# A transformer decoder on one core: scores kept together behind the outputs, paired projections later in their step

## The chip, the cores and the metric

The kernel runs on one core of one Trainium2 chip. The metric is the device time of one execution in microseconds (us). Several executions are timed, and their median is compared. One further execution is recorded by the hardware profiler. The core has five engines that run side by side, each with its own queue of instructions, which it takes in the built order: PE (TensorE, matrix products; its weight loads are shown as PEld), DVE (VectorE), ACT (ScalarE), POOL (GpSimd) and SP (SyncE, which issues DMA transfers). ACT issues transfers too. Results of PE land in PSUM banks, from where DVE or ACT copy them.

## The reference, cut to what matters

The program is a decoder of two layers on 8 sequences of 128 tokens with 512 features. The change lies in the last attention of it, the cross attention of layer 1, which is

```python
hidden = jnp.concatenate([context, latents], axis=1)       # 128 + 128 tokens
q = (latents @ Wq.T).reshape(b, q_len, H, HD)              # H = 16 heads of 96
k = (hidden @ Wk.T).reshape(b, s_len, KV, HD)              # KV = 4 groups
v = (hidden @ Wv.T).reshape(b, s_len, KV, HD)
...
scores = jnp.einsum('bkgqd,bksd->bkgqs', q, k) * scale
attn = jax.nn.softmax(scores.astype(jnp.float32), axis=-1).astype(q.dtype)
out = jnp.einsum('bkgqs,bksd->bkgqd', attn, v)
...
return out @ Wo.T
```

followed by `x = layernorm(x + ...)` and a low-rank mixture (`L1_ffn`), again with a residual and a norm.

## The kernel before, in words

The cross attention goes in steps, one for each sequence b (0 to 7), in the loop at line 1212. A step has two halves `hh` of 8 heads each. For each half it makes:

- the scores (`Heads8.__init__`, line 971): 24 matmuls of 32 x 128 by 256 columns in 6 rounds of four row groups, into two PSUM tiles of two banks each. PE runs each matmul as two instructions, so a half has 48. Both two-bank tiles are taken by one half.
- the softmax: maxima on DVE (`maxima`, line 986), exponentials on ACT (line 997), reciprocals, scaling and 32 x 32 transposes on DVE (`exps`, lines 1001 to 1005), in two sub-halves of four heads.
- the turn (`turn`, line 1011): 16 DMAs of 64 KB that bring the probabilities into the tile `pT`. The first half's go out on SP, the second half's on SP and ACT in turn.

The outputs of step b - 1 (`mixed`, line 1021) are computed in step b: three groups `o_x` of 8 matmuls, each into one bank, copied to `oTx` by DVE (groups 0 and 2) or ACT (group 1). There are four single banks, used by all results other than scores.

Between these, `Front` makes values (`pvx`), keys (`pkx`) and queries (`pqx`) of the next pair of sequences in pieces, which `nxt.go(n)` takes from a list. `LOWS` lists pieces of the low-rank mixture of earlier sequences.

The output projection of sequences 0 to 3 is done in pairs (`paired`, line 1043): sequences 0 and 1 in step 2, sequences 2 and 3 in step 4. Seven products of 6 matmuls (12 PE instructions) take the place of eight. In order: product 1 of the first operand, copied to `p1` by ACT (line 1073); product 2 of `s`, copied to `p5` by ACT (line 1074); product 3; product 4 of `s` after DVE has subtracted from it (line 1051); product 5 of a half of `oTx` after DVE has subtracted `s` from that; products 6 and 7. The weight blocks for the products, 42 blocks of 128 KB, stream through three slots of 1 MB (`w_X_o`): after the last block of a slot is read, ACT issues the load of the slot's next content (`stream`, line 945). Blocks 0 to 23 are there when the pair starts, 24 to 41 come during it; block 24 is the first of product 5. After the pair, the slots are filled for the next pair, or with the plain weights (`plain_outputs`, line 950) for the later sequences, which are projected one at a time (line 1038).

The order on each engine is made by a planner when the program is built: it takes the recorded work and may put an instruction ahead of others that were recorded before it, within the data dependences. `tc.issue_after(x)` is an order edge: what is recorded inside is not placed ahead of x. In the built order of before, in steps 2 and 4, the scores of the second half, which are recorded after the pair, stand partly ahead of it: one round's half between the first and second group of outputs, one between the second and third, one behind the third, and the other 18 of the 24 matmuls behind the seven products.

Of the kernel before, what the change touches and what calls it, by code (L numbers as in the profile page):

```python
# [18 lines left out]
B, S, D = 8, 128, 512  # L19
# [24 lines left out]
def decoder(ctx: ExitStack, tc: tile.TileContext, a: dict, out: bass.AP):  # L44
    nc = tc.nc
# [475 lines left out]
    for n, (p, f) in enumerate(steps):  # L521
# [4 lines left out]
        for j in range(2):  # L526
            toks = slice(j * P, (j + 1) * P)
            of = lambda i, w, p=p, f=f, j=j: vs[p, j][i].rearrange("p a x d -> p (a x d)")[:, f * w : (f + 1) * w]
            units.append((qT[:, toks], kbd[:, :, toks], lambda of=of: of(0, 192), lambda of=of: of(1, 128)))
        now = Heads16(ap, units, causal_bias, oTs[p][:, :, f, :], f"a0_{p}_{f}")  # L530
# [318 lines left out]
    front = Front(0)  # L849
    turned = prev = oT_before = None  # L850
    keys_late = []
    for b in range(B):
# [3 lines left out]
        for f in (0, 2):  # L856
# [4 lines left out]
            now = Heads16(ap, units, alibi_bias(f), oT[:, f : f + 2, :], f"a1_{b}_{f}", keys_late)  # L861
# [57 lines left out]
    def form_sums():  # L919
        for t in slots:  # L920
            b11, b12, b21, b22 = (t[:, j * 512 : (j + 1) * 512] for j in range(4))
            nc.vector.tensor_tensor(b11, b12, b11, ALU.subtract)
            nc.vector.tensor_tensor(b12, b22, b12, ALU.subtract)
            nc.vector.tensor_tensor(b22, b22, b11, ALU.subtract)
            nc.vector.tensor_tensor(b21, b21, b22, ALU.subtract)
# [28 lines left out]
    with stage("x1b", 2, side="right") as ap, stage("f1", 2, side="right") as fp:  # L954
# [60 lines left out]
        def mixed(b, v, pT, oT):  # L1015

            for n in range(NS):
                po = bank(f"o_x1_{b}_{n}")
                for s in range(2):
                    for g in range(KV):  # L1020
                        nc.tensor.matmul(  # L1021
                            po[32 * g : 32 * g + 32, :],
                            lhsT=v[:, s, g * XD + 32 * n : g * XD + 32 * n + 32],
                            rhs=pT[:, s].rearrange("p i h x -> p (i h) x")[:, :, 64 * g : 64 * g + 64],
                            start=(s == 0), stop=(s == 1),
                        )
                (nc.scalar.copy if n == 1 else nc.vector.tensor_copy)(  # L1027
                    oT[:, n, :].rearrange("p (h i t) -> p i h t", h=4, i=4),
                    po.rearrange("p (i h t) -> p i h t", i=4, h=4),
                )  # L1030
# [12 lines left out]
        def paired(b0, b1):  # L1043

            o0, o1 = oTs_x.pop(b0), oTs_x.pop(b1)
            x0, x1 = xs[b0], xs[b1]
            first, second = slice(0, 256), slice(256, 512)
            s = ap.tile([P, NS, 256], F32, tag="s", name=f"s_x1_{b0}", bufs=1)
            p1, p5 = (ap.tile([P, 256], F32, tag=f"p{i}", name=f"p{i}_{b0}", bufs=1) for i in (1, 5))
            r0, r1 = (xp.tile([P, D], F32, tag="x", name=f"x_x1_{b}") for b in (b0, b1))  # L1050
            add = lambda eng, o, l, r, op=ALU.add: eng.tensor_tensor(o, l, r, op)
            used = [0]

            def product(left):
                ps = bank(f"pox_{b0}_{used[0]}")[:, :256]
                for kk in range(6):
                    h, n = divmod(kk, NS)
                    t, u = divmod(used[0], 8)
                    nc.tensor.matmul(  # L1059
                        ps, lhsT=left[:, n, h * P : (h + 1) * P], rhs=slots[t % 3][:, u * 256 : (u + 1) * 256],  # L1060
                        start=kk == 0, stop=kk == 5,
                    )
                    used[0] += 1
                    if u == 7:
                        if t < 3:
                            stream(t + 3)
                        elif t < 5 and not paired.last:
                            stream(t - 3)
                return ps

            add(nc.vector, s, o1[:, :, first], o1[:, :, second])
            add(nc.vector, o1[:, :, first], o0[:, :, first], o1[:, :, first], ALU.subtract)
            nc.scalar.copy(p1, product(o0[:, :, first]))
            nc.scalar.copy(p5, product(s))
            add(nc.vector, s, s, o0[:, :, first], ALU.subtract)
            add(nc.vector, x0[:, first], x0[:, first], p1)
            add(nc.vector, r0[:, first], product(o0[:, :, second]), x0[:, first])
            add(nc.vector, o0[:, :, second], o0[:, :, second], s, ALU.subtract)
            add(nc.vector, p1, product(s), p1)
            add(nc.vector, x0[:, second], x0[:, second], p5)  # L1080
            add(nc.vector, x0[:, second], x0[:, second], p1)
            add(nc.vector, r0[:, second], product(o0[:, :, second]), x0[:, second])
            add(nc.vector, x1[:, second], x1[:, second], p5)
            add(nc.vector, p1, product(o1[:, :, first]), p1)
            add(nc.vector, x1[:, first], x1[:, first], p1)
            add(nc.vector, r1[:, second], x1[:, second], p1)
            add(nc.vector, r1[:, first], product(o1[:, :, second]), x1[:, first])
            if paired.last:
                plain_outputs()
            else:  # L1090
                stream(2)
            for b, r in ((b0, r0), (b1, r1)):
                mean, rs = moments(r, f"x1_{b}")
                nc.vector.tensor_scalar(r, r, mean, rs, ALU.subtract, ALU.mult)
                xs[b] = r
# [95 lines left out]
        def outputs(b):  # L1191
            oTs_x[b] = ap.tile([P, NS, 512], F32, tag="oT", name=f"oTx_{b}", bufs=2)
            mixed(b, vs_x.pop(b), pTs.pop(b), oTs_x[b])
# [9 lines left out]
        PAIRED = 4  # L1203
# [8 lines left out]
        for b in range(B):  # L1212
            pr, j = divmod(b, 2)
            if j == 0 and b:
                front, nxt = nxt, upcoming
            toks = slice(j * P, (j + 1) * P)
            for hh in range(2):
                now = Heads8(front.qT[:, :, toks], front.kT[:, :, :, toks], 2 * hh, f"x1_{b}_{hh}")
                now.maxima()
                now.exps(0)  # L1220
                now.exps(1)
                if b < B - 2 and hh == 0:

                    if b > PAIRED:
                        nxt.go((4, 3)[j] if b < B - 3 else 2)
                        mix(b - 1)
                    elif b and not j:
                        nxt.go(4)
                        outputs(b - 1)
                        paired.last = b == PAIRED  # L1230
                        paired(b - 2, b - 1)
                    else:
                        nxt.go((4, 3)[j])
                        if b:
                            outputs(b - 1)
                    pTs[b] = pT_tile(b)
                    now.turn(pTs[b])
                    if b < 2:
                        with tc.issue_after(now.exp.ins):
                            keep_sums() if b else bring_weights()  # L1240
                elif b < B - 2:
                    if j == 1 and b < B - 3:

                        upcoming = Front(pr + 2)
                    now.turn(pTs[b], (nc.sync, nc.scalar))
                    nxt.go(2)
                    if b < 2:
                        with tc.issue_after((now.exp if b else now.rows).ins):
                            if b:
                                for t in range(3):  # L1250
                                    stream(t)
                            else:
                                form_sums()
                    for piece in LOWS.get(b, ()):
                        piece()
                    if b < B - 3:
                        nxt.go((1, 2)[j])
                elif hh == 0:

                    if b == B - 2:  # L1260
                        front.go(3)
                    else:
                        projected(b - 2)
                    first = now
                else:
                    if b == B - 2:
                        low_turn(B - 6)
                        low_turn(B - 5)
                        outputs(b - 1)
                        low_last(B - 6)  # L1270
                        low_scores(B - 4)
                        low_last(B - 5)
                    else:
                        low_turn(B - 4)
                        outputs(b - 1)
                        low_tokens(B - 3)

                    pTs[b] = pT_tile(b)
                    for heads in (first, now):
                        heads.turn(pTs[b], (nc.sync, nc.scalar))  # L1280
            vs_x[b] = front.v[:, j]
# [240 lines left out]
```

## Time and profile before

| | |
|---|---|
| Median of 3 timed runs | 871.89 us (871.49 to 874.71) |
| The profiled execution | 871.16 us |
| Its span, first to last instruction | 869.4 us |
| Granted TensorE clock, mean | 0.996 of full |
| PE busy | 843.0 us, 97% of the span |
| Cross attention, step 2 | outputs from 605.12 us, pair from 613.09 to 631.42 us |
| Cross attention, step 4 | outputs from 693.22 us, pair from 701.24 to 719.57 us |

Times inside an execution count from the span's start. In a row of the timeline, the first number is the start, the second the length from the first start to the last end, then the engine (with a q behind it where its sequencer issues a DMA), the line, the operation, written and read tiles, shapes, the number of instructions and in brackets the idle time before it and what ended it. Matmuls overlap, so the distance from one start to the next is the price of a group, not its length. In a row of the windows, the columns are the stretch, its length, the busy time of PE, PEld, DVE, ACT and POOL with the number of instructions, the granted clock, the share of the DMA engines and GB/s.

### The profile page before, as it was taken

How to read it: one execution, taken by the hardware profiler on the slowest of the kernel's cores; microseconds unless marked ns; L12 is line 12 of the kernel's file. 1: busy time of each engine (PE TensorE's matmuls, PEld its weight loads, DVE VectorE, ACT ScalarE, POOL GpSimd, SP SyncE). 2: the span in 40 equal slices, each digit the busy share in tenths (PEclk: the TensorE clock that was granted, in tenths of full speed). 3: DMA queues.
4: the chain of work that ended last, by engine and by line, in shares of the span. 5: the costliest groups of instructions: out<-in, count | busy, mean ns of one | idle time of the engine just before them, and what ended most of it. 6: DMA issues, size and time to landing. Idle time of an engine off the chain costs nothing.

```text
span 869.4 us, 18203 instructions
## 1 busy us (share of the span) xinstructions
PE 843.0 (97%) x6554; PEld 538.6 (62%) x6554; DVE 562.4 (65%) x2252; ACT 365.4 (42%) x1531; POOL 202.3 (23%) x299
## 2 busy tenths in 40 slices
PE   9999999999899999999999999999999999999996
PEld 5776655655454455555555687875787677576454
DVE  3656687776868666777778512874565547458754
ACT  3876574654222136766666403142024202224310
POOL 2500243243535315555555300000000000000000
PEclk9999999999999999999999999999999999999999
DMA  8700000130300002000002001676652264322341
GB/s 329 310 2 26 2 13 14 50 110 4 143 13 0 25 0 98 2 1 2 2 2 76 2 25 58 189 230 179 197 165 58 55 165 169 82 58 49 88 95 37
DMA packets 35258, 67.99 MB, mean 78 GB/s; under 512 B 5984, under 2 KB 22496, under 8 KB 32992
## 3 DMA queue, kind: packets, MB, share of 16 engines
q1 hardware_dynamic: 23152, 41.13, 15.3%
q10 hardware_dynamic: 12016, 25.70, 9.6%
q8 instruction: 52, 0.85, 0.4%
q14 instruction: 38, 0.31, 0.1%
HBM read 44.78 MB, written 5.24 MB: 58 GB/s over the span
## 4 chain that ended last, share of the span: by engine, by line
PE 59%; DVE 21%; ACT 11%; POOL 3%; issue 2%; DMA 2%; SPq 1%; ACTq 1%; POOLq 0%; DVEq 0%
ACT e_a L197 6%; PE pqx L86 6%; PE pkx L86 4%; PE pvx L86 4%; PE pox L1059 4%; PE o_x L1021 4%; PE pq L86 4%; DVE e_a L184 3%; PE pk L86 3%; PE pv L86 3%; PE po L86 3%; PE s_x L976 3%; PE pt_a L228 2%; PE pox L1038 2%; PE pof L623 2%
## 5 line engine op out<-in xcount | busy, mean ns | idle before, releaser
L197 ACT ACTIVATE e_a<-e_a,m_a 128x128 f32<-128x128 f32 (+1 forms) x512 | 184.8, 364 | 98.4 <-DVE m_a L184 98.4
L997 ACT ACTIVATE e_x<-s_x,m_x 128x256 f32<-128x256 f32 x128 | 58.6, 485 | 123.2 <-DVE m_x L987 66.9
L197 ACT ACTIVATION_READ_ACCUMULATOR e_a<-e_a,m_a 128x1 f32 x512 | 97.1, 190 | 0.0
L86 PE MATMUL pqx<-xTx,w_X_q 128*128 128x256 f32 x384 | 85.0, 380 | 1.3 <-DVE rc L1123 1.3
L86 PEld LDWEIGHTS pqx<-xTx,w_X_q 128*128 128x128 f32 x384 | 72.5, 190 | 12.6 <-issue 3.0
L97 POOL TENSOR_TENSOR rs_x<-ve_x,neghalf 128x1 f32<-128x1 f32 x7 | 3.8, 547 | 274.2 <-DVE ve_x L95 255.2
L986 DVE TENSOR_REDUCE m_x<-s_x 128x4 f32<-128x1024 f32 x32 | 37.6, 1218 | 38.8 <-PE s_x L976 38.8
L211 POOL TENSOR_TENSOR e_a<-e_a,rc_a 128x512 f32<-128x512 f32 (+1 forms) x64 | 52.7, 845 | 35.1 <-DVE rc_a L208 18.8
L228 PE MATMUL pt_a<-ident,e_a 128*128 128x128 f32 x384 | 48.4, 273 | 2.3 <-DVE m_a L184 2.3
L228 PEld LDWEIGHTS pt_a<-ident,e_a 128*128 128x128 f32 x384 | 43.5, 140 | 11.2 <-issue 4.7
L976 PE MATMUL s_x<-kTx,qTx 32*128 32x256 f32 x768 | 50.0, 384 | 0.0
L184 DVE CUSTOM_DVE_ANT_0 e_a<-s_a,masks 128x128 f32<-128x128 f32 (+1 forms) x256 | 46.8, 253 | 4.7 <-PE s_a L165 3.3
L184 DVE CUSTOM_DVE_ANT_0 e_a<-s_a,alibi 128x128 f32<-128x128 f32 (+1 forms) x256 | 47.3, 253 | 1.4 <-PE s_a L165 1.3
L976 PEld LDWEIGHTS s_x<-kTx,qTx 32*128 32x128 f32 x768 | 39.0, 184 | 14.5 <-issue 11.6
L1021 PE MATMUL o_x<-pT_x,vx 128*32 128x512 f32 x384 | 43.7, 595 | 0.9 <-DVE oTx L1027 0.4
L184 DVE DVE_READ_ACCUMULATOR2_ANT m_a<- 128x1 f32 x512 | 42.5, 83 | 0.0
L1005 DVE STREAM_TRANSPOSE e_x<-e_x 128x1024 f32<-128x1024 f32 x32 | 39.7, 1241 | 0.9
L1004 DVE TENSOR_SCALAR e_x<-e_x,rc_x 128x256 f32<-128x256 f32 x128 | 36.3, 348 | 3.5 <-DVE rc_x L1001 1.8
L165 PEld LDWEIGHTS s_a<-kbd,qT 32*64 32x64 f32 x1024 | 20.9, 131 | 27.9 <-issue 15.4
L165 PE MATMUL s_a<-kbd,qT 32*64 32x128 f32 (+1 forms) x1024 | 33.4, 334 | 1.5 <-ACT pT_a L229 1.0
L843 ACT COPY qTx<-pqx 128x512 f32<-128x512 f32 x24 | 13.7, 599 | 49.9 <-PE pqx L86 38.9
L86 PE MATMUL pq<-xT,w_L_Wq 128*128 128x256 f32 x128 | 32.4, 395 | 0.0
(255 smaller groups left out, 1687.5 us busy)
## 6 DMA issues: line engine op xcount, KB each, us to landing
pT_x<-e_x SPq DMA_DIRECT2D x176, 64.0 KB, 2.1
pT_x<-e_x ACTq DMA_DIRECT2D x80, 64.0 KB, 2.3
w_X_q<-in_X_q SPq DMA_DIRECT2D x3, 1024.0 KB, 4.7
w_X_o<-in_X_ot ACTq DMA_DIRECT2D x3, 1024.0 KB, 8.2
ts<-w_X_o ACTq DMA_DIRECT2D x3, 1024.0 KB, 6.6
w_X_o<-in_X_ob ACTq DMA_DIRECT2D x4, 768.0 KB, 5.6
w_X_o<-ts ACTq DMA_DIRECT2D x6, 512.0 KB, 5.9
w_X_o<-in_X_o ACTq DMA_DIRECT2D x3, 1024.0 KB, 5.5
```

The source lines that it names most:

```text
L86: nc.tensor.matmul(ps, lhsT=l, rhs=r, start=(i == 0), stop=(i == n - 1))
L165: nc.tensor.matmul(s[r // 2][64 * u : 64 * u + 64, r % 2, cols], lhsT=qT[rows, 64 - 64 * part : P - 64 * part], rhs=kbd[rows, :, :keys], s ...
L184: self.scored = nc.vector.tensor_tensor_reduce(self.e[:, r, cols], s[i][:, r % 2, cols], bias(r, cols), -1.0, 3e38, ALU.add, ALU.min, self ...
L197: nc.scalar.activation(e[:, r, x, :], e[:, r, x, :], AF.Exp, scale=-1.0, bias=self.m[:, part, r, x : x + 1], accum_out=self.su[:, part, r, ...
L211: nc.gpsimd.tensor_tensor(e, e, bc(self.rc[:, part, rs, :].unsqueeze(3), list(e.shape)), ALU.mult)
L228: nc.tensor.transpose(pt[:, r, cols], self.e[:, 2 * i + r, cols], ident)
L976: nc.tensor.matmul(sc[g // 2][:, g % 2, u * 256 : (u + 1) * 256], lhsT=qT[rows, (h0 + u) * NS + n, :], rhs=kT[rows, n], start=(n == 0), st ...
L986: nc.vector.tensor_reduce(m, self.s[i], AX.X, ALU.max, negate=True)
L997: self.exp = nc.scalar.activation(self.e[:, :, j, :], self.s[half][:, i, :].rearrange("p (a k) -> p a k", k=32), AF.Exp, bias=self.m[:, j ...
L1004: nc.vector.tensor_scalar(e, e, self.rc[:, j : j + 1], None, ALU.mult)
L1005: self.rows = nc.vector.transpose(self.e[:, :, js, :], self.e[:, :, js, :])
L1021: nc.tensor.matmul(po[32 * g : 32 * g + 32, :], lhsT=v[:, s, g * XD + 32 * n : g * XD + 32 * n + 32], rhs=pT[:, s].rearrange("p i h x -> p ...
```

## The change

The handles of the last output matmul and the last product matmul are kept (`mixed.done`, `paired.done`). Scores get order edges: those of the second half in steps 1 to 5 behind the step's outputs, those of the first half in steps 3 and 5 behind the pair of the step before. In steps 2 and 4 the pair is no longer recorded in the first half of the step, after the outputs, but in the second half, after the softmax of the second half and ahead of its turn. The pieces of `Front` at the end of a second half go ahead of the low-rank pieces.

```diff
@@ mixed
-                        nc.tensor.matmul(
+                        mixed.done = nc.tensor.matmul(
@@ paired, product
-                    nc.tensor.matmul(
+                    paired.done = nc.tensor.matmul(
@@ the loop over b
             for hh in range(2):
-                now = Heads8(front.qT[:, :, toks], front.kT[:, :, :, toks], 2 * hh, f"x1_{b}_{hh}")
+                behind = mixed if b and hh and b < B - 2 else paired if not hh and b in (3, 5) else None
+                with tc.issue_after(behind.done.ins) if behind else nullcontext():
+                    now = Heads8(front.qT[:, :, toks], front.kT[:, :, :, toks], 2 * hh, f"x1_{b}_{hh}")
                 now.maxima()
                 now.exps(0)
                 now.exps(1)
@@
                     if b > PAIRED:
                         nxt.go((4, 3)[j] if b < B - 3 else 2)
                         mix(b - 1)
-                    elif b and not j:
-                        nxt.go(4)
-                        outputs(b - 1)
-                        paired.last = b == PAIRED
-                        paired(b - 2, b - 1)
                     else:
                         nxt.go((4, 3)[j])
                         if b:
@@
                         upcoming = Front(pr + 2)
+                    if b and not j:
+                        paired.last = b == PAIRED
+                        paired(b - 2, b - 1)
                     now.turn(pTs[b], (nc.sync, nc.scalar))
                     nxt.go(2)
@@
+                    if b < B - 3:
+                        nxt.go((1, 2)[j])
                     for piece in LOWS.get(b, ()):
                         piece()
-                    if b < B - 3:
-                        nxt.go((1, 2)[j])
```

## The prediction

> **What bounds the kernel now.** I read the page first: which engine has no slack, and what the last chain is made of.
>
> ```profile
> PE 843.0 (97%) x6554; PEld 538.6 (62%) x6554; DVE 562.4 (65%) x2252; ACT 365.4 (42%) x1531; POOL 202.3 (23%) x299
> PE 59%; DVE 21%; ACT 11%; POOL 3%; issue 2%; DMA 2%; SPq 1%; ACTq 1%; POOLq 0%; DVEq 0%
> ```
>
> PE has 26 us of idle time in 869, and none worth a name between 613 and 690 us: a microsecond in which PE waits there is a microsecond of the end. So the question is only what PE waits for in steps 2 and 4. Second, the chain of waits through step 2 (start, length, what):
>
> ```profile
> 605.19 1.90 PE o_x L1021 x16
> ...
> 607.11 0.70 DVE oTx L1027
> ...
> 607.86 1.97 PE o_x L1021 x16
> ...
> 609.85 0.59 ACT oTx L1027
> ...
> 610.49 1.97 PE o_x L1021 x16
> ...
> 612.48 0.57 DVE vx L820
> ...
> 613.09 18.40 PE pox L1059 x84
> 631.49 2.36 PE s_x L976 x36
> ```
>
> Each group of outputs starts 0.04 to 0.06 us after the copy of the group before it (the three value tiles hold the other single banks), and the first product 0.05 after a copy of values. The 12 scores that the built order puts between them are not in the chain: they fill three waits of 0.7 us. Only the 36 behind the products cost time, 631.42 to 633.77. Third, the timeline of VectorE, start and length first:
>
> ```profile
> 615.66 0.96 DVE L1051 TENSOR_TENSOR oTx<-oTx,oTx 128x768 f32<-128x768 f32 x1
> ...
> 618.57 0.96 DVE L1051 TENSOR_TENSOR s_x<-s_x,oTx 128x768 f32<-128x768 f32 x1 [1.62 <-PE pox L1059]
> ...
> 621.50 0.95 DVE L1051 TENSOR_TENSOR oTx<-oTx,s_x 128x768 f32<-128x768 f32 x1
> ...
> 634.27 2.35 DVE L986 TENSOR_REDUCE m_x<-s_x 128x4 f32<-128x1024 f32 x2
> ...
> 638.77 0.18 DVE L1001 RECIPROCAL rc_x<-su_x 128x4 f32<-128x4 f32 x1 [1.49 <-ACT e_x L997]
> 639.18 1.14 DVE L1004 TENSOR_SCALAR e_x<-e_x,rc_x 128x256 f32<-128x256 f32 x4 [0.22 <-DVE rc_x L1001]
> 640.35 1.25 DVE L1005 STREAM_TRANSPOSE e_x<-e_x 128x1024 f32<-128x1024 f32 x1
> ```
>
> The operand of product 4 is written at 618.57 and that of product 5 at 621.50, each over 1 us before its product (620.96, 623.55). The softmax of the second half comes after all products. Last, ScalarE, two rows of the DMA issues of 600 to 660 us, and two stretches with their throughput:
>
> ```profile
> 615.98 0.37 ACT L1073 COPY p<-pox 128x256 f32<-128x256 f32 x1 [5.55 <-PE pox L1059]
> 615.99 0.34 ACTq L945 DMA_DIRECT2D w_X_o<-in_X_ob  x1
> ...
> 636.81 0.47 ACT L997 ACTIVATE e_x<-s_x,m_x 128x256 f32<-128x256 f32 x1 [17.87 <-DMA w_X_o<-in_X_ob]
> ```
>
> ```profile
> w_X_o<-in_X_ob ACTq DMA_DIRECT2D x2, 768.0 KB, 5.7
> pT_x<-e_x ACTq DMA_DIRECT2D x8, 64.0 KB, 2.3
> ```
>
> ```profile
> 580.00:600.00 20.00, 18.60 (x121) 15.16 (x120) 8.12 (x19) 8.27 (x29) 0.00 (x0) 1.00 0.77 205
> 620.00:640.00 20.00, 20.00 (x115) 16.40 (x114) 11.37 (x28) 3.19 (x15) 1.09 (x2) 1.00 0.84 270
> ```
>
> Slot 0 is loaded again as soon as its blocks are read (615.99); product 5 needs it.
>
> **The change part by part.** The built order shows where it acts: on PE only steps 2 and 4 differ, and there the 24 scores of the second half stand in one block between the outputs and the products. The other edges (second halves of 1, 3, 5; first halves of 3 and 5) move nothing on PE: cost 0. I follow step 2 in the clock of the trace of before.
>
> *Scores.* The outputs still wait for the same copies, so they start at 605.12, 607.86 and 610.49 and end at 612.34; the two gaps are idle instead of filled. A block of all 48 score instructions takes 2.80 us to the next start (644.33 to 647.14), so the products start at 615.14. Before, 36 of them cost 2.35 (631.42 to 633.77). Products 1 to 3 last 7.87 (613.09 to 620.96): 623.01.
>
> *VectorE.* Its order is now: copies, s, oTx (free at 616.53, as before), two reductions, and then the softmax with the paired operands between its two halves. From the rows of the second half: exponentials 2.54 after the start of the reductions (634.27 to 636.81), the first reciprocal 1.96 later, the scaling 0.41 later, the transpose 1.17 later, the second reciprocal 1.17 later (641.52), the next instruction 0.06 later. So the operand of product 4 starts at 616.53+2.54+1.96+0.41+1.17+1.17+0.06 = 623.84 and ends at 624.80; product 4 starts at 624.86. **First wait: 1.85 us.** It ends 2.59 later (620.96 to 623.55), at 627.45. Behind it VectorE has scaling 1.17, an addition 0.4, the transpose 1.17 and an addition out of PSUM 0.36, from 624.72 (starts are 0.88 apart behind that operation): the operand of product 5 starts at 627.82 and ends at 628.77, product 5 starts at 628.83. **Second wait: 1.38 us.** Three products of 7.87: 636.70. Before, PE was at that point at 633.77: **+2.93 us**.
>
> *ScalarE and the weights.* The copies p1, p5 and the weight loads now stand behind eight exponentials: 616.53+2.54 = 619.07, and 3.76 for eight (636.81 to 640.57): 622.83 instead of 615.99. The first 768 KB land 5.7 later, at 628.5, 0.3 before product 5 wants them. The 256 and 512 KB behind them, wanted at 632.3, and the next 512 KB, wanted at 634.0, come at 270 GB/s by 631.4 and 633.3 (cost 0), at 205 GB/s by 632.3 and 634.9 (0.9 late). So the bounds are 0 and 0.9 us a step; I take 0.2, since the stretch with this very stream had 270.
>
> *Turns.* The eight DMAs on SP start after the transpose at 627.5 instead of 644.6. The eight on ACT now stand behind the loads for the next pair, and some wait for such a load to land: six loads of 3 MB in all (three slots of 1 MB), from 633 to 635 on, end at 645 to 650 by the two throughputs, and the last turn lands 2.3 later, at 653 at the latest. The reader, the outputs of step 2, stood at 657.69 and stands 3 later: 7 us of cover. If it is gone, each us is lost on PE. The exponentials of step 3, queued behind these issues, need maxima of scores that end at 650 and cannot start before 652 anyway. POOL runs one small power twice a step (0.55), after 4.7 us of idle time: 0.
>
> *Pieces before low-rank work.* Same instructions, next to each other. In step 4 a transpose waited 0.38 for a copy of kTx (730.49); two transposes and a matmul now stand between: -0.4 at best, -0.3 taken. In step 3 both orders find their operands ready: 0.
>
> **Sum.** Step 4 repeats step 2 to 0.01 us, 88.15 later (products 701.24, values 721.93). 2 x (2.93 + 0.2) - 0.3 = +6.0. The profiled execution took 871.16 (span 869.4), so 877.1; it stands 0.73 under the median of 871.89. On the median: **877.8 us**, slower by 0.7%.
>
> [...] Row: the 12 scattered scores occupy PE from 606.97 to 613.09 in three pieces of 0.75 to 0.89 to the next start, 12 of a block take 0.70. [...] The chain, in which each piece ends on a copy, says that this time is not to be had. Row: PE waited 1.40 before the values at 597.18, and the 16 matmuls behind took 5.43 against 5.33 elsewhere, at a granted clock of 1.00. [...]
>
> **The rivals.**
> - *Faster: packing pays.* If outputs found a free bank, the 12 scores would cost what a block costs, and a step would give 2.42 - 0.70 for them: 2 x 1.7 less, 868.4. It decides only if VectorE also has the operand of product 4 by 623.0; by its rows it is 1.85 late. For it: a block's price of 58 ns. Against it: the copies in the chain.
> - *Weights late.* If loads take 1 us more to land, with the turn DMAs of 64 KB beside them, products 5 to 7 wait 1 to 2 us more a step: 880 to 882. For it: 0.3 us of margin. Against it: the turns of the first half are issued by 622.7 (16 at 0.64 from 612.47), before the loads start.
> - *No change.* The waits are repaid, because the second half's softmax no longer runs into step 3 (scores wait there for exponentials). That needs a wait of PE in step 3 or 5 that goes; the timeline shows PE without a gap from 613 to 695 and only the 0.38 in step 4: 871.5 to 874.
>
> **How the numbers follow.** Forecast 0.69 (own range 875.5 to 879.5), weights late 0.14, no change 0.11, faster 0.06. The range of 873.8 to 881.5 leaves out faster, most of no change and the end of weights late. About 0.5%, 4.4 us, is what can be told from no change: slower needs 876.3, so 0.64 + 0.14 = 0.78; same 0.05 + 0.11 = 0.16; faster 0.06.
>
> **What would show it.** In the profile after: outputs at the same starts with idle gaps of 0.8 in place of the scores; a gap of 1.9 before product 4 ended by s on VectorE and of 1.4 before product 5, twice; copies of p behind the exponentials; turns landed long before the outputs. I am wrong if PE runs the seven products without a gap, if product 5 waits for a DMA, or if a gap of step 3 or 5 takes time back.

## The result and the profile after

The changed kernel took 879.69 us (median of 7 runs, 876.54 to 880.97), the kernel before, run beside it, 872.78 (871.49 to 875.48). The ratio is 1.0066, with a 95% interval of 1.0044 to 1.0087: slower by 0.7%, against a forecast of 877.8 us. The profiled execution of the changed kernel took 879.69 us too, with a span of 877.9. Medians of the kernel before differ from one group of runs to the next (872.8 to 874.4), so ratios below are always to the runs of the same group.

The page of the changed kernel, busy times and the last chain:

```profile
PE 842.1 (96%) x6554; PEld 539.0 (61%) x6554; DVE 562.4 (64%) x2252; ACT 365.4 (42%) x1531; POOL 202.7 (23%) x299
PE 57%; DVE 21%; ACT 11%; POOL 3%; DMA 3%; issue 2%; SPq 2%; ACTq 1%; DVEq 0%; POOLq 0%
```

PE has as much work as before, but 36 us of idle time in its span instead of 26. The starts of PE's groups say where the 8.5 us between the two spans lie (each stretch runs from one start to the next; "values" are those behind the last product of the pair, the last boundary is the scores of the second half of step 5):

| Stretch | before | changed | difference | forecast |
|---|---|---|---|---|
| span start to first output of step 2 | 605.12 | 608.42 | +3.30 | 0 |
| step 2: first output to values | 28.65 | 31.72 | +3.07 | +3.13 |
| to first output of step 4 | 59.45 | 59.33 | -0.12 | 0 |
| step 4: first output to values | 28.71 | 31.54 | +2.83 | +3.13 |
| to the scores in step 5 | 39.15 | 38.37 | -0.78 | -0.3 |
| to the end of the span | 108.32 | 108.52 | +0.20 | 0 |

PE's timeline through step 2 of the changed kernel:

```profile
608.42 1.92 PE L1021 MATMUL o_x<-pT_x,vx 128*32 128x512 f32 x16
611.16 1.92 PE L1021 MATMUL o_x<-pT_x,vx 128*32 128x512 f32 x16 [0.81 <-DVE oTx L1027]
613.79 1.92 PE L1021 MATMUL o_x<-pT_x,vx 128*32 128x512 f32 x16 [0.71 <-ACT oTx L1027]
615.65 2.87 PE L976 MATMUL s_x<-kTx,qTx 32*128 32x256 f32 x48
618.45 2.86 PE L1059 MATMUL pox<-w_X_o,oTx 128*128 128x256 f32 x12
621.14 2.75 PE L1059 MATMUL pox<-w_X_o,s_x 128*128 128x256 f32 x12
623.74 2.75 PE L1059 MATMUL pox<-w_X_o,oTx 128*128 128x256 f32 x12
628.53 2.86 PE L1059 MATMUL pox<-w_X_o,s_x 128*128 128x256 f32 x12 [2.04 <-DVE s_x L1051]
632.29 8.01 PE L1059 MATMUL pox<-w_X_o,oTx 128*128 128x256 f32 x36 [0.90 <-issue]
```

The waits of PE in the changed kernel between 600 and 770 us (us in all, how often, longest):

```profile
PE pox L1059 <- DVE s_x L1051: 3.9, 2, 2.0
PE pox L1059 <- issue: 1.8, 2, 0.9
PE o_x L1021 <- DVE oTx L1027: 1.6, 2, 0.8
PE o_x L1021 <- ACT oTx L1027: 1.5, 2, 0.8
```

The outputs start as far apart as before (2.74 and 2.63 us), with idle gaps where the scores were. A product is 2.59 us from the next start, so product 4 (628.53) is 2.20 late and product 5 (632.29) is 1.17 late; in step 4 it is 1.98 and 1.17. VectorE shows what they wait for:

```profile
624.39 0.18 DVE L1001 RECIPROCAL rc_x<-su_x 128x4 f32<-128x4 f32 x1 [2.00 <-ACT e_x L997]
625.15 1.14 DVE L1004 TENSOR_SCALAR e_x<-e_x,rc_x 128x256 f32<-128x256 f32 x4 [0.58 <-DMA pT_x<-e_x]
626.33 1.25 DVE L1005 STREAM_TRANSPOSE e_x<-e_x 128x1024 f32<-128x1024 f32 x1
627.49 0.14 DVE L1001 RECIPROCAL rc_x<-su_x 128x4 f32<-128x4 f32 x1
627.55 0.93 DVE L1051 TENSOR_TENSOR s_x<-s_x,oTx 128x768 f32<-128x768 f32 x1
628.39 1.14 DVE L1004 TENSOR_SCALAR e_x<-e_x,rc_x 128x256 f32<-128x256 f32 x4
...
629.77 1.24 DVE L1005 STREAM_TRANSPOSE e_x<-e_x 128x1024 f32<-128x1024 f32 x1
630.94 0.39 DVE L1051 TENSOR_TENSOR x_x<-pox,x_a 128x256 f32<-128x256 f32 x1
631.25 0.94 DVE L1051 TENSOR_TENSOR oTx<-oTx,s_x 128x768 f32<-128x768 f32 x1
```

The operand of product 4 ends at 628.48, that of product 5 at 632.19, each just ahead of its product. The waits view puts the second wait to "issue", but the row of its operand ends 0.10 us before product 5 starts. Last, ScalarE:

```profile
622.43 0.48 ACT L997 ACTIVATE e_x<-s_x,m_x 128x256 f32<-128x256 f32 x1 [8.69 <-DVE m_x L987]
...
623.84 0.33 ACTq L945 DMA_DIRECT2D w_X_o<-in_X_ob  x1
...
625.59 0.51 ACT L997 ACTIVATE e_x<-s_x,m_x 128x256 f32<-128x256 f32 x1
...
626.04 0.41 ACT L1073 COPY p<-pox 128x256 f32<-128x256 f32 x1
```

The copy to p1 comes behind the eight exponentials, as forecast. The weight load does not: it goes out at 623.84, in the middle of them.

### The profile page after: what moved, and what is told of

Same layout as the page of the kernel before. It is cut to its first block, busy times and chain, and to the rows that moved or that the text cites. A ratio compares the mean times of both kernels' runs of the same rounds, so it can differ in the third digit from the quotient of the medians.

```text
span 877.9 us, 18202 instructions
## 1 busy us (share of the span) xinstructions
PE 842.1 (96%) x6554; PEld 539.0 (61%) x6554; DVE 562.4 (64%) x2252; ACT 365.4 (42%) x1531; POOL 202.7 (23%) x299
## 4 chain that ended last, share of the span: by engine, by line
PE 57%; DVE 21%; ACT 11%; POOL 3%; DMA 3%; issue 2%; SPq 2%; ACTq 1%; DVEq 0%; POOLq 0%
ACT e_a L197 6%; PE pqx L86 6%; PE pkx L86 5%; PE pvx L86 5%; PE o_x L1021 4%; PE pq L86 3%; DVE e_a L184 3%; PE pk L86 3%; PE pv L86 3%; PE po L86 3%; PE pox L1059 2%; PE s_x L976 2%; PE pt_a L228 2%; PE pox L1038 2%; PE pof L623 2%
## 5 line engine op out<-in xcount | busy, mean ns | idle before, releaser
L976 PE MATMUL s_x<-kTx,qTx 32*128 32x256 f32 x768 | 46.6, 383 | 0.0
```

Source lines behind the costliest of these rows:

```text
L976: nc.tensor.matmul(sc[g // 2][:, g % 2, u * 256 : (u + 1) * 256], lhsT=qT[rows, (h0 + u) * NS + n, :], rhs=kT[rows, n], start=(n == 0), st ...
```

## The experiments

My theory: VectorE's softmax, now between the operands of the paired products, is the loss. Rivals: the order edges, late weights, a new wait elsewhere. Step 2 and step 4 below are the stretches of the table above, from the first output to the values; the stretch behind step 4 is the row "to the scores in step 5".

**1. The edges alone.** The kernel before, with the edges and nothing else of the change:

```diff
-                now = Heads8(...)
+                behind = mixed if b and hh and b < B - 2 else paired if not hh and b in (3, 5) else None
+                with tc.issue_after(behind.done.ins) if behind else nullcontext():
+                    now = Heads8(...)
```

> The kernel before with the order edges on the scores alone; the paired projections and the pieces of the low-rank work stay where they were. Nothing is left out. Theory (the VectorE order is what costs, and the scores kept together cost only what they lose as fillers): the two gaps between the groups of outputs of steps 2 and 4 stand idle for 0.7 to 0.8 us each, and the block of 48 scores takes 2.87 us where the 36 that cost time took 2.35, so 0.5 us more in each of two steps, 1.0 us in all: 1.001 of the kernel before (+0.5 to +1.5 us). Products run without a gap, as before. Rival, the edges are the cost: +6 to +7 us, 1.007 to 1.008. Rival, scores kept together pay: each of the four breaks taken out of the outputs saves about 0.2 us or more, -1 to -4 us, 0.995 to 0.999.

Measured: 0.9997 of the kernel before (0.9982 to 1.0012). Steps 2 and 4 took 29.09 and 29.14 us, 0.44 and 0.43 more; the stretch behind step 4 took 38.73, 0.42 less, which I had not expected. The edges are not the loss. (The edges only hold the scores behind the outputs: four of the 48 score instructions still stand between outputs and products, the rest behind the products.)

**2. The late pair without the edges.**

```diff
-                behind = mixed if b and hh and b < B - 2 else paired if not hh and b in (3, 5) else None
-                with tc.issue_after(behind.done.ins) if behind else nullcontext():
-                    now = Heads8(...)
+                now = Heads8(...)
```

> The changed kernel without the order edges on the scores: the paired projections still come late, recorded behind the maxima and exponentials of the second half. Nothing is left out. Theory (the place of the softmax on VectorE costs): products 4 and 5 of steps 2 and 4 still wait for VectorE, about 2.0 and 1.2 us, since the softmax still stands ahead of their operands; the scores fill the gaps between the outputs again and start the whole chain 0.5 us earlier, so the time is 0.5 to 1.5 us below that of the changed kernel, 1.005 to 1.006 of the kernel before. Rival, the edges are the cost: back to the time of the kernel before within 1 us.

Measured: 1.0062 (1.0043 to 1.0081). Against the edges as cause, this settles it: the loss is there without them. But steps 2 and 4 took 33.02 and 32.86 us, 1.3 longer each than in the changed kernel, not 0.5 shorter. The wait for VectorE grew (2.48 and 2.25) by what PE gained: product 4 of step 2 starts 20.10 us behind the first output, in the changed kernel 20.11; and product 4 took 4.35 us where it takes 2.86. The windows of this kernel around that product (stretch, length, PE busy, granted clock, DMA share, GB/s):

```profile
624.00:627.00 3.00, 1.10 (x5) 1.00 1.04 353
627.00:630.50 3.50, 3.50 (x10) 0.51 0.84 209
630.50:634.00 3.50, 3.50 (x16) 1.00 1.02 312
```

Behind the wait the granted clock was 0.51 over 3.5 us. In the changed kernel's own profile it was 1.00 from 625 to 634 us, through both of its waits.

**3. The softmax behind the pair.** The changed kernel, with only this moved:

```diff
                 now.maxima()
-                now.exps(0)
-                now.exps(1)
+                late = hh and b in (2, 4)
+                if not late:
+                    now.exps(0)
+                    now.exps(1)
@@
                         paired(b - 2, b - 1)
+                    if late:
+                        with tc.issue_after(paired.done.ins):
+                            now.exps(0)
+                            now.exps(1)
```

> The changed kernel with one thing moved: in steps 2 and 4 the exponentials, the scaling and the transposes of the second half come behind the last product of the pair (the maxima stay ahead). Nothing is left out. Theory (VectorE's softmax between the paired operands is the whole of the loss): the waits ahead of product 4 (2.20 and 1.98 us in the changed kernel) and product 5 (1.17 and 1.17 us) go to under 0.3 us each, 5.5 to 6.5 us come back, and the time is 873 to 874.5 us where the kernel before is at 872.3: 1.001 to 1.003. Rival, the weights are late: product 5 then waits for a DMA, and at least 2 us of the loss stay. Rival, a new wait takes the place: the turn of the second half is issued about 13 us later, and the outputs of the next step, at 664 us, wait for its last transfer; then the products run without a gap, but the outputs of steps 3 and 5 start late by up to 5 us and the time stays at that of the changed kernel.

Measured: 1.0046 (1.0024 to 1.0068), times from 873.6 to 881.9. PE's timeline of this kernel in step 2 and, last row, behind step 4:

```profile
617.70 2.86 PE L1059 MATMUL pox<-w_X_o,oTx 128*128 128x256 f32 x12
620.39 2.75 PE L1059 MATMUL pox<-w_X_o,s_x 128*128 128x256 f32 x12
622.98 2.75 PE L1059 MATMUL pox<-w_X_o,oTx 128*128 128x256 f32 x12
625.57 2.75 PE L1059 MATMUL pox<-w_X_o,s_x 128*128 128x256 f32 x12
628.16 7.93 PE L1059 MATMUL pox<-w_X_o,oTx 128*128 128x256 f32 x36
635.93 2.74 PE L86 MATMUL pvx<-w_X_v,xTx 128*128 128x384 f32 x8
...
736.72 1.13 PE L1163 MATMUL pof<-wf,lT 128*128 128x512 f32 x2 [1.78 <-ACT lT L1158]
```

Both waits are gone: steps 2 and 4 take 28.26 and 28.31 us, together 6.7 less than in the changed kernel and 0.8 less than before. So the softmax between the operands is what the two steps lost. The whole did not follow, because another wait came: the turn of step 4 goes out later, and the copy to lT (an operand of the low-rank pieces) stands behind eight of its DMAs on ScalarE's queue. In whole times this version can't be told from the changed kernel: the two intervals overlap, and the profiled execution (875.01) is the third fastest of twelve. Experiments 7 and 12 answer in whole times. Product 5 starts at 628.16, with no wait for a weight load.

**4. Late in step 2 alone.**

```diff
                         if b:
                             outputs(b - 1)
+                        if b == 4:
+                            paired.last = b == PAIRED
+                            paired(b - 2, b - 1)
@@
-                    if b and not j:
+                    if b == 2:
```

> The changed kernel with the paired projections late in step 2 alone; in step 4 they stand ahead of the scores again as in the kernel before, but with the edges. Nothing is left out. Theory (each step costs by itself, nothing is given back between): step 2 from the first output to the next values keeps its 31.7 us (28.65 in the kernel before), step 4 falls from 31.5 us to 29.0 to 29.4, so 2.1 to 2.6 us less than the changed kernel: 1.003 to 1.005 of the kernel before. Rival, the loss is made once (a late start of step 2 that is carried on): the time stays within 0.7 us of the changed kernel. Rival, only step 4 costs in the end (step 2 is given back in its later part): back within 1 us of the kernel before.

Measured: 1.0104 (1.0084 to 1.0123), slower than the changed kernel, which no theory had. Step 4 fell to 29.14 us as expected. The stretch behind it rose to 45.75 us. ScalarE's timeline there:

```profile
738.88 5.81 ACTq L1011 DMA_DIRECT2D pT_x<-e_x  x8
744.74 0.28 ACT L1158 ACTIVATE lT<-pt_lT 128x128 f32<-128x128 f32 x1 [9.89 <-DMA pT_x<-e_x]
```

With the pair early, the turn comes late, and with the pieces moved nothing of PE's is left to do meanwhile: PE waited 4.23 us for lT, and the two matmul instructions behind took 2.08 us, where they take 1.11 in the changed kernel. Two parts of the change need each other here: with the pair early and the pieces in the old order (experiment 1), the copy to lT goes ahead of the turn's issues, and PE does not wait for it.

**5. The low-rank pieces ahead again.**

```diff
-                    if b < B - 3:
-                        nxt.go((1, 2)[j])
                     for piece in LOWS.get(b, ()):
                         piece()
+                    if b < B - 3:
+                        nxt.go((1, 2)[j])
```

> The changed kernel with the pieces of the low-rank work ahead of the pieces of the next pair again, as in the kernel before. Nothing is left out. From the values of step 4 to the second block of scores of step 5 the changed kernel takes 38.37 us, the kernel before 39.15, and the edges alone 38.73. Theory (the order of the pieces gives back 0.4 us, and the rest of the 0.8 us comes from the late pair): 38.5 to 39.0 us in that stretch, the time 0.2 to 0.7 us above that of the changed kernel, with the waits ahead of products 4 and 5 as there. Rival, the whole 0.8 us comes with the order of the pieces: 39.15 us. Rival, the pieces ahead find the scalar engine's queue still full of the turn (its last issue is at 736.4 us in the changed kernel, the first piece that needs that engine at 740.8): a wait of 1 to 4 us ahead of the pieces' second product, and 39.5 to 42.5 us.

Measured: 1.0070 (1.0046 to 1.0094), not to be told from the changed kernel's 1.0066. The stretch behind step 4 took 38.68 us: the order of the pieces is worth 0.31, the other 0.47 comes with the rest, and experiment 1 had 0.42 of it with the edges alone.

**6. The gap ahead of step 2.** In the kernel before, the second turn of step 1 through SP alone:

```diff
-                    now.turn(pTs[b], (nc.sync, nc.scalar))
+                    now.turn(pTs[b], (nc.sync,) if b == 1 else (nc.sync, nc.scalar))
```

The 3.3 us ahead of step 2 lie at the values, at 597 us. This is PE's row there in the kernel before:

```profile
597.18 5.43 PE L86 MATMUL pvx<-w_X_v,cT 128*128 128x384 f32 x16 [1.40 <-ACT qTx L843]
```

The same row of the changed kernel:

```profile
598.79 7.12 PE L86 MATMUL pvx<-w_X_v,cT 128*128 128x384 f32 x16 [2.77 <-ACT qTx L843]
```

Of experiment 4:

```profile
599.84 5.43 PE L86 MATMUL pvx<-w_X_v,cT 128*128 128x384 f32 x16 [3.40 <-ACT qTx L843]
```

And of experiment 5:

```profile
599.03 7.12 PE L86 MATMUL pvx<-w_X_v,cT 128*128 128x384 f32 x16 [3.42 <-ACT qTx L843]
```

The gap (1.40 to 3.42 us) and the length of the 16 matmul instructions behind it vary: 5.43 us at a granted clock of 1.00 (the kernel before, 596 to 604 us; experiment 4, 600 to 604), 7.12 where it was 0.53 (the changed kernel, 599.5 to 603) or 0.50 (experiment 5, 600 to 603), though PE's instructions up to there are the same in all four.

> The kernel before with one thing changed ahead of the place of the change: the second turn of step 1 goes through SP's queue alone, not through SP and the scalar engine. Nothing is left out. Theory (the 3.3 us by which the changed kernel was late ahead of step 2, and the spread of the times from 870 to 877 us in both kernels, come from the gap ahead of the values, which is 1.40 to 3.40 us long in the profiles because the copies to qTx stand behind 8 turns and 5 weight loads on the scalar engine's queue, and after a gap of over 2 us the granted clock is often 0.5 for 3.4 us, 1.7 us lost): the gap goes to under 0.5 us, the granted clock stays at 1.00, the time falls by 1.5 to 4 us, 0.996 to 0.998 of the kernel before, and the times lie within 2.5 us of each other. Rival, the turn lands too late: 16 transfers of 0.64 us on SP, landed at 600 us, against the outputs at 603.7; if the outputs wait, the gap has only moved. Rival, the clock is not bound to the gap: the times spread as before.

Measured: 0.9979 (0.9965 to 0.9994), 11 of 12 times between 870.4 and 872.7, one at 874.2. The gap is gone, and the granted clock was 1.00 from 590 to 610 us. Part of it came back as the rival had it: the outputs waited 1.23 us for the turn.

**7 to 11. Taking the remaining waits away.** Experiment 7 is experiment 3 with the second turns of steps 1 and 4 on SP:

```diff
-                    now.turn(pTs[b], (nc.sync, nc.scalar))
+                    now.turn(pTs[b], (nc.sync,) if b in (1, 4) else (nc.sync, nc.scalar))
```

> The version with the softmax behind the pair, with the second turns of steps 1 and 4 through SP's queue alone. Nothing is left out. Theory (what is left of the loss there is no longer the pair, but two waits for copies of the scalar engine that stand behind its share of a turn: the one ahead of the values of step 2, 2.32 us and 1.7 us of clock, and the one ahead of the second product of the pieces in step 4, 1.78 us, which the version has and the changed kernel has not): both go, steps 2 and 4 stay at 28.3 us, the stretch behind step 4 falls from 40.9 to 38.4 us or less, and the time is 867 to 870 us, 0.993 to 0.996 of the kernel before. Rival, SP becomes the bound: its turns of steps 4 and 5 pile up and the outputs of step 4 wait for the last transfer; then 871 to 874 us.

Measured: 0.9962 (0.9947 to 0.9977), 870.42 us, all ten times from 869.5 to 871.2, faster than the kernel before by 0.4%. The wait for lT is gone (stretch behind step 4: 38.37). The outputs of step 2 wait 1.83 for the turn. Experiment 8 takes this version and splits the values around the outputs, with 4 of the 16 transfers of step 1 on ScalarE:

```diff
-                        nxt.go((4, 3)[j])
+                        nxt.go(2 if b and not j else (4, 3)[j])
                         if b:
                             outputs(b - 1)
+                        if b and not j:
+                            nxt.go(2)
```

> The version before this one (softmax behind the pair, the turn of step 4 on SP alone, that of step 1 on SP but for 4 of 16 transfers), with one value group ahead of the outputs of steps 2 and 4 and two behind them, where all three stood ahead. Nothing is left out. Theory (the outputs wait 0.8 and 0.7 us because the three value tiles hold the other single banks): with one value tile ahead two more banks are free, the two gaps go in each step, and the time falls by 2 to 3 us more, to 865 to 868 us, 0.990 to 0.994 of the kernel before. Rival, VectorE's order is what delays the copies, not the banks: the values behind wait for copies instead, and the time is that of the version before this one. Rival, the outputs, now 5.3 us earlier, wait for the turn of the step before (last landing about 597.5 us against a start at 598.5): up to 2 us lost in step 2 alone.

Measured: 0.9978 (0.9964 to 0.9991). Step 4 did what was expected: its outputs ran in 5.36 us without a gap. Step 2 lost that and more: its outputs waited 4.45 us for a transfer of the turn and then took 7.78 us. That the weight loads, now issued early, ran beside the turn and delayed it is my estimate; no view of this run shows it. PE's row of the outputs there:

```profile
604.26 7.78 PE L1021 MATMUL o_x<-pT_x,vx 128*32 128x512 f32 x48 [4.45 <-DMA pT_x<-e_x]
```

Experiment 9 leaves the values where they were and the turn of step 1 on both queues (that of step 4 stays on SP), and puts the weight loads of step 1 behind the last copies to qTx (`Front.copied` is the handle of that copy):

```diff
-                            if b:
-                                for t in range(3):
-                                    stream(t)
...
+                    if b == 1:
+                        with tc.issue_after(Front.copied.ins):
+                            for t in range(3):
+                                stream(t)
```

> The version with the softmax behind the pair and the turn of step 4 on SP alone; the second turn of step 1 goes through both queues as in the kernel before, but the five weight loads that stood ahead of the last copies to qTx on the scalar engine now come behind them. Nothing is left out. Theory (the gap ahead of the values of step 2 is made by the loads, not by the turn, and the loads that run beside a turn delay its landing): the copies come about 2 us earlier, the gap falls from 1.4 to 3.4 us to under 0.6 us at a granted clock of 1.00, and the outputs of step 2 do not wait for a transfer, where they waited 1.83 us with the turn on SP alone: 868 to 869.5 us against 870.4 there, 0.993 to 0.996 of the kernel before. Rival, the eight turns alone hold the copies: a gap of 1 us or more stays, and so does the spread.

Measured: 0.9952 (0.9936 to 0.9968), 868.83 us. No gap ahead of the values, no wait for a turn; but the first copy of outputs came later (1.07 instead of 0.81), and products waited 0.51 for p and 0.25 for a weight load. Experiment 10 adds the split of experiment 8:

> The version before this one with one value group ahead of the outputs of steps 2 and 4 and two behind them. Nothing is left out. Theory (the gaps of 0.8 and 0.7 us between the outputs come from the single banks that the three value tiles hold; in the earlier try of the split step 4 ran its 48 output matmuls in 5.36 us without a gap, and step 2 lost 4.45 us to a turn that landed beside weight loads): both steps run their outputs in 5.36 us, 1.8 us less in each, 864 to 866.5 us, 0.989 to 0.992 of the kernel before. Rival, the turn of step 1 lands too late again: outputs of step 2 wait for a DMA by 1 us or more, and the time is 866.5 to 869 us.

Measured: 865.01 us (864.57 to 866.78), 0.9907 (0.9890 to 0.9924), the best of all. PE's timeline in its step 2:

```profile
595.55 2.75 PE L86 MATMUL pvx<-w_X_v,cT 128*128 128x384 f32 x8
598.23 5.36 PE L1021 MATMUL o_x<-pT_x,vx 128*32 128x512 f32 x48
603.76 2.85 PE L86 MATMUL pvx<-w_X_v,cT 128*128 128x384 f32 x8 [0.18 <-DVE oTx L1027]
606.45 2.74 PE L86 MATMUL pvx<-w_X_v,xTx 128*128 128x384 f32 x8
609.12 2.87 PE L976 MATMUL s_x<-kTx,qTx 32*128 32x256 f32 x48
611.92 2.86 PE L1059 MATMUL pox<-w_X_o,oTx 128*128 128x256 f32 x12
```

One wait of 0.18 is left between 590 and 770 us. Experiment 11 makes the same two edits in the kernel before, pair early and no edges:

> The kernel before, pair early and without edges, with the same two edits: weight loads behind the last copies to qTx in step 1, and one value group ahead of the outputs of steps 2 and 4, two behind them. Nothing is left out. It tells whether the late pair has a part in the gain. Theory (with the gaps between the outputs gone the scores are no longer wanted as fillers; the late pair with the softmax behind it saves only the breaks between scores and other matmuls, 0.39 us per step in the profiles, and the order of the pieces 0.4 to 0.8 us): this one is 1 to 2 us above the version before it, 866 to 868 us, 0.991 to 0.994 of the kernel before. Rival, the late pair is what pays: 870 us or more. Rival, it does nothing: the same time within 0.7 us.

Measured: 865.86 us (864.91 to 867.09), 0.9914 (0.9897 to 0.9931). The difference of 0.85 us to experiment 10 is smaller than the spread of either, and lies between my theory (1 to 2) and the rival (under 0.7): whether the late pair has a part in the gain stays open. In the profiles step 4 from its first value to those behind the pair is the same (34.36 and 34.26); in step 2 the values behind the outputs wait 1.05 us for a copy in experiment 11 and 0.18 in experiment 10.

**12. The changed kernel without the gap ahead of step 2.** The edit of experiment 9 in the changed kernel:

> The changed kernel with one edit ahead of step 2: the five weight loads of step 1 come behind the last copies to qTx, as in the two versions before. Nothing is left out. It separates what the change costs from the gap ahead of step 2, whose length varies. Theory (of the 8.5 us between the two profiled spans 3.3 are the gap and its half clock, and steps 2 and 4 with the stretch behind them are 5.0): the gap is gone, the outputs of step 2 start at 603.5 to 604 us, steps 2 and 4 keep 31.5 to 31.8 us with the waits of 2.0 to 2.2 and 1.2 us, and the time is 874 to 876 us; the version with the softmax behind the pair and the same edit took 868.8, so the softmax between the paired operands is worth 5.5 to 6.5 us. If half clock follows a wait of 2 us in a run, 1.5 us more per step. Rival, the gap and the loss in steps 2 and 4 are bound to each other (a later start made the waits shorter): the waits grow by what the start gains, and the time stays at 877 us or more.

Measured: 876.38 us, 1.0027 (1.0015 to 1.0038). The gap is gone, and the outputs of step 2 start at 604.67. Part of the rival came true: the second output waits 1.68 instead of 0.81 for the copy ahead of it. Product 4 of step 2 took 4.51 us here, with the granted clock at 0.83 from 624 to 628 us and 0.74 from 628 to 632, so step 2 took 33.11; step 4 took 31.54 with the waits of the changed kernel. The time lies between my theory (874 to 876) and the rival (877 or more). Experiment 9 has the same edit ahead of step 2, the softmax behind the pair and the turn of step 4 on SP, and took 0.9952. The two intervals are apart, so in whole times the softmax between the operands costs about 0.75%, or 6.5 us, with the lower clock behind its waits in some executions (product 4 in 4.51 us instead of 2.86).

## Why the prediction was right, and where its sizes were off

- *PE is the bound, the scattered scores are free.* Right. Experiment 1: without them as fillers a step costs 0.44 us more, not less.
- *Scores: the outputs keep their distances, products start 2.05 later.* Right: 10.03 us from the first output to the first product, against 7.97 before.
- *First wait 1.85.* The mechanism was right (experiment 3), the size was off: 2.20 in step 2 and 1.98 in step 4. In step 2 the scaling began 0.76 behind the reciprocal and not 0.41; the profile names a transfer of the turn of the first half.
- *Second wait 1.38.* It was 1.17, since product 4 ended later. With the first, 3.37 and 3.15 instead of 3.23.
- *Weights 0.2 a step.* Mis-sized; 0. I had put the loads behind eight exponentials because they stand behind them in the built order; ScalarE issued them among these. The first landed at 628.80, 3.5 us before product 5 and not 0.3. PE waited for them only in a version whose products do not wait for the softmax (0.25 us, experiment 9).
- *Turns cost 0.* Right for the changed kernel, where ScalarE's eight issues of step 4 end 4.4 us before its copy to lT. Experiments 3 and 4 are what happens when that cover is gone: 1.78 and 4.23 us of PE.
- *Pieces -0.3.* The order of the pieces gave 0.31 (experiment 5). The stretch gave 0.78; I did not foresee that the rest comes with the other edits.
- *Ahead of step 2: nothing.* In the profiles 3.30 us lie there. The change moves no instruction there, and the gap stands behind ScalarE's DMA issues of step 1 (in the changed kernel the last ends at 598.11, and the copies to qTx start at 598.15; experiments 6, 9 and 12 take the gap away). The five profiled kernels with the edges and this order of issues had gaps of 2.32 to 3.42 us, the two without edges 1.40 and 1.99; with one profile of each, it stays open whether that is chance. The whole times of experiment 1 speak for chance: it has the edges and took 0.9997 of the kernel before, though its profiled execution (875.67 us, the third slowest of twelve) reached the outputs of step 2 3.90 us later than that of the kernel before.
- *The sum.* It was 6.0 for the parts that the change touches, and the profiles have 5.2 there (8.5 with the 3.3). The medians are 6.9 apart, because the profiled execution of the kernel before stands 1.6 below its median. That they came within 1 us of the sum is in part luck: the parts were put 0.8 too high, and the time ahead of step 2 was not in the sum.
- *The clock.* The sum has nothing for a lower clock behind the two waits, and the changed kernel's profile shows none (1.00 from 625 to 634 us, a wait of 2.04 in it). Other profiles show one: behind the same wait of 2.04 us product 4 took 4.52 us in experiment 4 and 4.51 in experiment 12, for 2.86 (last section).
- *Scores in one block.* The version of experiment 3, with one block and no wait of the products, needs 28.26 us for step 2, and experiment 1, with 4 score instructions apart, 29.09. Where these 0.83 us go is not shown by any run. In the change as it stood, with the waits, step 2 took 31.72.

## What to carry to other kernels

When work on the bounding engine is moved, follow the order on the engines that feed it: here a softmax with its eight exponentials slipped between two short subtractions, and 3.2 to 3.4 us a step went to waiting for these. Fillers between waits cost nothing here (a step takes 0.44 us more without them, experiment 1); a better gain was to take the waits away, by freeing PSUM banks ahead of the outputs (two of three value groups moved behind them: 48 output instructions in 5.36 us without a gap, experiment 10), and to keep copies that PE waits for from standing behind a run of DMA issues (no gap ahead of the values in experiment 9, 1.40 us in the kernel before).

## What the runs showed of the hardware that was not expected

- The granted clock fell to 0.5 behind some idle times of PE, and not behind others of the same length. Behind a wait of 2.04 us the 12 instructions of product 4 took 4.52 us in experiment 4 (granted clock 0.50 from 629 to 632 us) and 4.51 in experiment 12 (0.83 from 624 to 628, 0.74 from 628 to 632), but 2.86 in the changed kernel (1.00 from 625 to 634). Behind the gap ahead of step 2 the 16 value instructions took 7.12 us in experiment 5 (3.42 us of gap, then 0.50 from 600 to 603), but 5.43 in experiment 4 (3.40 us of gap, then 1.00 from 600 to 604). So one and the same wait cost 1.7 us more in one execution and nothing more in another; what decides it is not shown.
- ScalarE's queue issued DMAs that stand behind exponentials in the built order while these were still running (623.84, with the last exponential at 625.59, in the changed kernel). Its copies came behind the DMA issues ahead of them: eight issues of a turn took 5.41 us (experiment 9) to 7.45 (the changed kernel), and in experiment 4 the copy to lT started at 744.74, behind eight that went out from 738.88 to 744.69.
